# Multiplying feed-forward 0's first gate block for three token tiles before the fourth is turned

## The chip, the core and the metric

The kernel runs on one core of a Trainium2 chip. The metric is device time in microseconds (us), the median of the runs; smaller is better. The work is spread over TensorE (PE in the profile; PEld is its weight load), VectorE (DVE), ScalarE (ACT), GpSimd (POOL) and the DMA queues, which SyncE (SP) issues to here.

## What is computed

Two batches of 512 tokens, 512 channels wide, go through four layers, each in the form x = x + layernorm(layer(layernorm(x))). Only the first two matter here. Cut to them:

```python
# layer 0: a state space model, 1024 channels x 16 states, over 512 time steps
state = state * exp(dt_t * A) + (dt_t * u_t) * B_t      # for every t
y     = sum over the 16 states of state * C_t
y     = (y + x * D) * silu(gate);  out = y @ W_out.T
x     = x + layernorm(out)

# feed-forward 0: weights unpacked from 4-bit words, 512 -> 1376 -> 512
h     = layernorm(x)
inter = silu(h @ Wg) * (h @ Wu);   out = inter @ Wd
x     = x + layernorm(out)
```

Attention and a second feed-forward with latent experts follow. All matrix products are in f32.

## The kernel before

**The scan stage.** A batch is held as four token tiles of 128 tokens. The state space model is computed by blocks of 128 channels, eight for each batch, and for two of the 16 states at a time. That gives 16 blocks times 8 pairs of states, 128 steps, numbered s in the loop at L1152; gi is the pair within a block. A step has on DVE times_B (L1092, makes the input of step s+1), then scan (L1096, the recurrence); on ACT exps (L1076, the decay of step s+2, into one of two buffers `das`); on POOL times_C (L1102, and for some steps L1104, which adds the two states into one); and on PE sums (L1124), which adds up the states by products with the identity, two steps later. With gi of 2, fin (L1130) takes the sum of the block before, on DVE.

**Work beside the scan.** While batch 1 is scanned, PE also does batch 0's way out of the layer and its feed-forward 0 up to the product gate times up. This is a generator, `stream` (L1030). Out of it come, in this order: the output projection (`out_tiles`, L990), the turning of the normalised rows into channels by transposes (`turned`, L832), and `ffn0` (L1012). `ffn0` goes over 11 blocks of 128 columns. For each it multiplies gate (fg) and then up (fu), with four matmul calls each, since 512 channels are four chunks of 128. A call of f32 is two PE instructions.

**A plan written at trace time.** The order of instructions on PE, ACT, DVE and POOL is that in which the Python code issues them: `pin` (L407) ties every instruction to the one before it on its engine. The order comes from bookkeeping in the loop. Every step gives PE a credit of STEP = 3.5, of which at most MM = 0.86 is carried over from the step before (L1155). `sums` costs 0.86 for each product, a matmul call of the stream 0.86, a tile's transposes 0.43. While credit is above zero, the loop takes the next piece from the generator; a piece that has to wait yields `None`, and then nothing more is taken in that step.

**Jobs and ticks.** What follows a product on the other engines is a job, started with `spawn(job, lag)` and run when the count `now` has gone on by the lag. A step has two ticks: the first comes before times_B, the second between times_B and scan. So a job that runs in the second tick of step s puts its DVE instruction just ahead of scan(s), and its ACT instructions just ahead of exps(s+2). The jobs that matter:

- `turned`'s `out` (L843): the copy of one turned tile from the PSUM bank into hT, on ACT; lag 1 for the last two tiles.
- `ffn_gate_job` (L1000), after fg with lag 2: three ACT instructions by `silu_of` (L722 to L724), then a step later one POOL product (L727), which sets `st["it", i]`.
- `ffn_up_job` (L1006), after fu with lag 2, and not before `st["it", i]` + 2: one DVE product (L1009), called it(i) below.

**Banks.** PE's products of the stream share two PSUM banks in turn (`bank`, L738): one is given only when the last but one taken has been released. `dt_job` (pv, once for each block) takes a turn as well.

**Weights.** `gu_weights` (L366) loads 256 columns of gate and of up, 512 KB each, on SP's queue into a ring of three buffers. SP is not one of the pinned engines.

Of the kernel before, what the change touches and what calls it, by code (L numbers as in the profile page):

```python
# [18 lines left out]
P = 128  # L19
B = 2  # L20
S = 512
H = 512
NT = B * S // P
TB = S // P
KH = H // P
# [31 lines left out]
def tile_sandwich(  # L57
# [5 lines left out]
    nc = tc.nc  # L63
# [300 lines left out]
    hTs, o16 = {}, {}  # L364

    def gu_weights(b, j):  # L366
        cols = slice(j * PW, min((j + 1) * PW, INTER))
        n = cols.stop - cols.start
        return [w4(wgu_d[:, a, :, cols], f"w{nm}{b}_{j}", KH, n) for a, nm in enumerate("gu")]
# [29 lines left out]
    def xT_tile(name):  # L399
        return xTp.tile([P, KH, S], F32, tag="xT", name=name)  # L400
# [27 lines left out]
    with ExitStack() as mamba:  # L428
# [41 lines left out]
        def w_in(part, b, c):  # L470

            key = "w", part, b, c // 2
            if key not in st:
                st[key] = w4(W_in[part * NCH // 2 + c // 2], f"w_{'xg'[part]}{b}_{c // 2}")
            return st[key]
# [103 lines left out]
        with ExitStack() as p1:  # L579
# [5 lines left out]
            def bank1(i, name):  # L585
                return mbank(name) if i % 2 else ps_1.tile([P, S], F32, tag="mm", name=name)
# [3 lines left out]
            for i in range(TB + 2):  # L590
# [4 lines left out]
                if 0 <= i - 1 < TB:  # L595
                    j = i - 1
# [18 lines left out]
            for c in range(NCH):  # L615
                w = w_in(0, 0, c)
                ps = bank1(c, f"px0_{c}")
# [65 lines left out]
        with ExitStack() as p2:  # L683
# [13 lines left out]
            for n in range(NG):  # L697
                nc.tensor.matmul(
                    B0[:, n, :], pick[R_B : R_B + N_ST, n, :], st["bc"][R_B : R_B + N_ST],
                    start=True, stop=True,  # L700
# [7 lines left out]
            def spawn(gen, lag=0):  # L708
                jobs.append([now[0] + lag, gen])
# [25 lines left out]
            def release(name):  # L735
                next(t for t in turns if t[0] == name)[1] = now[0]

            def bank(name):  # L738
                while not bank_free():
                    yield None  # L740
                turns.append([name, None])
                return mbank(name)

            MM = 0.86
# [14 lines left out]
            def gate(b, c):  # L759
                w = w_in(1, b, c)  # L760
                if c + 2 - c % 2 < NCH:
                    w_in(1, b, c + 2 - c % 2)
                if (b, c) == (0, 1):
                    turns.append([f"pg{b}_{c}", None])
                    ps = first_gate
                    yield from in_proj(b, ps, w, c % 2, KH - 1)
                else:
                    ps = yield from bank(f"pg{b}_{c}")
                    yield from in_proj(b, ps, w, c % 2)
                spawn(gate_job(b, c, ps), 2)  # L770
# [16 lines left out]
            def proj_x(c):  # L787
                w = w_in(0, 1, c)
                if c + 2 - c % 2 < NCH:
                    w_in(0, 1, c + 2 - c % 2)  # L790
                while now[0] < 2 * (NGI * (c - 3) + 4):
                    yield None
                ps = yield from bank(f"px1_{c}")
                yield from in_proj(1, ps, w, c % 2)
                spawn(x_job(c, ps), 2)

            def until(key, lag):
                while st.get(key, 1 << 30) + lag > now[0]:
                    yield None
# [29 lines left out]
                    st[name, i] = now[0]  # L829
                    st[name, i, "xn"] = xn  # L830

            def turned(name, dst):  # L832

                for i in range(TB):
                    lag = 1 if name == "f0" and i >= TB - 2 else 2
                    yield from until((name, i), lag)
                    tp = yield from bank(f"tp_{name}_{i}")
                    tp = tp.rearrange("p (k t) -> p k t", k=KH)
                    for kc in range(KH):
                        nc.tensor.transpose(tp[:, kc, :], st[name, i, "xn"][:, ts(kc, P)], ident)  # L840

                    def out(i=i, tp=tp):
                        nc.scalar.copy(dst[:, :, ts(i, P)], tp)  # L843
                        release(f"tp_{name}_{i}")
                        st[name, i, "free"] = st[name, "out"] = now[0]
                        yield 1

                    spawn(out(), lag)
                    yield MM / 2
                for i in range(TB):  # L850
                    while (name, i, "free") not in st:
                        yield None

# [8 lines left out]
            def ranks1():  # L862
                yield from until(("u1", NCH - 1), 3)
                pm = yield from bank("psm1")
                pm = pm[:, : TB * N_ROW].rearrange("p (i r) -> p i r", i=TB)
                for i in range(TB):
                    for c in range(NCH):
                        ranks_of(1, c, i, pm)
                        if c % 4 == 3:
                            yield MM  # L870
                spawn(ranks1_job(pm), 2)

            def rows1():
                yield from until("nb1", 1)
                pt = yield from bank("pt1")
                ranks_rows(1, pt)

                def out():
                    ranks_out(1, pt)
                    release("pt1")  # L880
                    st["rows1"] = now[0]
                    yield 1

                spawn(out(), 2)
                yield MM / 2
# [66 lines left out]
            def fc1_expert():  # L952

                fT = w4(fc1_wT.rearrange("p k (a n) -> p (k a) n", n=PW), "wf1T")
                fT = fT.rearrange("p (k a) n -> p k (a n)", k=LAT // P)
                ex = w4(expert_w, "wex", LAT // P, LAT)
                for a in range(KH // 2):
                    ps = yield from bank(f"pfe{a}")
                    for e in range(2):
                        for k in range(LAT // P):  # L960
                            nc.tensor.matmul(
                                ps[:, ts(e, LAT)], fT[:, k, ts(2 * a + e, P)], ex[:, k, :],
                                start=(k == 0), stop=(k == LAT // P - 1),
                            )
                        yield MM

                    def out(a=a, ps=ps):
                        t_ = trow(f"fe{a}")
                        nc.scalar.copy(t_, ps)
                        release(f"pfe{a}")  # L970
                        nc.sync.dma_start(
                            out=wfe_d[:, 2 * a : 2 * a + 2, :].rearrange("p k n -> p (k n)"), in_=t_
                        )
                        yield 1

                    spawn(out(), 2)
# [35 lines left out]
            def ffn0():  # L1012

                hT = hTs["f", 0]
                wt = {0: gu_weights(0, 0)}
                for i, m in enumerate(IC):
                    j, e = divmod(i, 2)
                    for a, job in enumerate((ffn_gate_job, ffn_up_job)):
                        ps = yield from bank(f"f{'gu'[a]}0_{i}")
                        for kc in range(KH):  # L1020
                            nc.tensor.matmul(  # L1021
                                ps[:m], wt[j][a][:, kc, e * P : e * P + m], hT[:, kc, :],
                                start=(kc == 0), stop=(kc == KH - 1),
                            )
                            yield MM
                        spawn(job(i, ps), 2)
                    if not e and j + 1 < NP:
                        wt[j + 1] = gu_weights(0, j + 1)

            def stream():  # L1030
                for c in range(1, NCH):
                    yield from gate(0, c)
                xT.append(xT_tile("xT1"))
                w_in(0, 1, 0)
                yield from turned("n1", xT[1])
                for c in range(NCH):
                    yield from proj_x(c)
                yield from until("words", 2)
                yield from gate(1, 0)
                yield from gate(1, 1)  # L1040
                yield from ranks1()
                yield from gate(1, 2)
                yield from gate(1, 3)
                yield from rows1()
                for c in range(NCH - 4, NCH):
                    yield from gate(1, c)
                yield from fc1_expert()
                yield from out_tiles()
                hTs["f", 0] = xT_tile("hT_f0")
                yield from turned("f0", hTs["f", 0])  # L1050
                yield from ffn0()

            def words_job():
# [144 lines left out]
        with ExitStack() as p3:  # L1198
# [9 lines left out]
            for j in range(NCH // 2):  # L1208
                w = wo_pair(1, 0, j)
                for e in range(2):  # L1210
                    c = 2 * j + e
                    for i in range(TB):
                        nc.tensor.matmul(
                            po[i], g[1][c][:, ts(i, P)], w[:, e, :],
                            start=(c == 0), stop=(c == NCH - 1),
# [9 lines left out]
            for i, m in enumerate(IC):  # L1225
                j, e = divmod(i, 2)
# [7 lines left out]
                for t in range(TB):  # L1234
                    nc.tensor.matmul(  # L1235
                        fo[t], its[i][:m, ts(t, P)], w[:m, e],
                        start=(i == 0), stop=(i == len(IC) - 1),
# [279 lines left out]
```

## Time and profile before

| what | value |
|---|---|
| runs, us | 950.59, 951.03, 942.81; median 950.59 |
| the profiled execution, us | 950.37 |
| its span, first to last instruction, us | 948.4 |
| mean granted TensorE clock | 0.964 of full |
| busy share of the span: PE, DVE, ACT, POOL | 91%, 71%, 45%, 51% |
| scan stage, about 76 to 570 us: PE, DVE, POOL busy | 450.25, 472.83, 387.12 of 494 us |
| first products of feed-forward 0 (fg, fu at L1021) | 405.3 us to 559.7 us |

The profile is of one execution, 950.37 us by its own clock with a span of 948.4 us. A row of the timeline has start, length, engine, line, operation, output and inputs, shapes, count, and in brackets the idle time of the engine before it with what ended it. A row that merges pipelined matmuls is a little longer than the work in it, since the end of the last is modelled: eight instructions that start 0.43 us apart show as 3.60 us. Busy shares are averages over stages that have different limits, so a change in one stage has to be read in that stage.

### The profile page before, as it was taken

Reading aid. Unit: us, or ns where it says so; the run is one execution under the profiler, and the core shown is the slowest. Engines: PE = TensorE matmul, PEld = TensorE weight load, DVE = VectorE, ACT = ScalarE, POOL = GpSimd, SP = SyncE. Lnnn points to the kernel's source line nnn. Section 1 sums busy time; section 2 is a strip of 40 time slices with the busy share of each in tenths; the row PEclk is TensorE's granted clock in tenths of the full one; section 3 lists DMA queues with packets and bytes.
Section 4 is the critical chain, followed back from the end, with each engine's and each line's share of the span. In section 5 each row is a group of like instructions: output and inputs, shape, how many; then the busy total and the mean of one; then the engine's idle time right before and its main releaser. Section 6 shows DMA issues by size and latency. Waiting matters only on the chain.

```text
span 948.4 us, 7168 instructions
## 1 busy us (share of the span) xinstructions
PE 862.0 (91%) x2188; PEld 386.8 (41%) x2188; DVE 670.2 (71%) x770; ACT 428.9 (45%) x654; POOL 487.1 (51%) x356
## 2 busy tenths in 40 slices
PE   6988978879999898799999989899999998999994
PEld 3433433323534343244444434345344444545441
DVE  5878999999999999999999976425600034525235
ACT  4367875665667655655656520215220014322122
POOL 7747887776887788767878774510000000011012
PEclk9998999889999999799999999999999999999998
DMA  6549011110004944000111013346113221100101
GB/s 206 197 145 361 22 45 31 38 38 23 23 25 158 320 154 155 22 22 23 44 45 31 17 61 125 105 139 220 56 48 88 57 88 46 66 12 22 56 0 44
DMA packets 43816, 80.08 MB, mean 84 GB/s; under 512 B 7774, under 2 KB 20937, under 8 KB 43778
## 3 DMA queue, kind: packets, MB, share of 16 engines
q1 hardware_dynamic: 41506, 73.64, 23.6%
q0 software_dynamic: 1984, 5.47, 1.6%
q10 hardware_dynamic: 288, 0.52, 0.2%
q8 instruction: 17, 0.28, 0.1%
q14 instruction: 21, 0.17, 0.1%
HBM read 68.37 MB, written 11.24 MB: 84 GB/s over the span
## 4 chain that ended last, share of the span: by engine, by line
PE 35%; DVE 31%; issue 14%; POOL 6%; ACT 5%; DMA 2%; SPq 1%; DVEq 0%; POOLq 0%; ACTq 0%
DVE bx L1096 12%; DVE bx L1092 9%; PE pup L1382 5%; PE py L1124 4%; PE fu L373 4%; PE fg L373 4%; PE pd L1445 4%; PE fo L1298 3%; DVE u L485 2%; POOL bx L1102 2%; PE fo L1235 2%; PE po L990 2%; PE pg L749 1%; PE pr L1413 1%; POOL w_d L329 1%
## 5 line engine op out<-in xcount | busy, mean ns | idle before, releaser
L1102 POOL TENSOR_TENSOR bx<-bx,C 128x1024 f32<-128x1024 f32 x128 | 302.5, 2364 | 102.5 <-DVE bx L1096 81.4
L1096 DVE TENSOR_TENSOR_SCAN bx<-da,bx 128x1024 f32<-128x1024 f32 x128 | 291.7, 2279 | 2.8 <-ACT da L1076 2.8
L1124 PE MATMUL py<-bx,ident 128*128 128x512 f32 x480 | 233.5, 615 | 26.1 <-POOL bx L1102 23.6
L1076 ACT ACTIVATE da<-dt,A 128x511 f32<-128x511 f32 x256 | 176.6, 691 | 146.9 <-DVE bx L1096 142.4
L1092 DVE TENSOR_TENSOR bx<-du,B 128x1024 f32<-128x1024 f32 x127 | 152.9, 1204 | 2.1 <-DVE du L1090 0.4
L1124 PEld LDWEIGHTS py<-bx,ident 128*128 128x128 f32 x480 | 91.1, 195 | 150.8 <-issue 96.4
L1311 DVE TENSOR_TENSOR it<-it,fu 128x512 f32<-128x512 f32 (+1 forms) x11 | 7.6, 688 | 77.4 <-PE fu L373 76.3
L387 POOL TENSOR_TENSOR sd<-ve,half 128x4 f16<-128x4 f16 x2 | 2.1, 1044 | 115.0 <-DVE ve L385 115.0
L749 PE MATMUL pg<-xT,w_g 128*128 128x512 f32 x114 | 56.0, 621 | 3.3 <-ACT dt L573 3.3
L1382 PE MATMUL pup<-hT_l,wup 128*128 128x512 f32 x128 | 57.2, 602 | 0.0
L1445 PE MATMUL pd<-wdn,hid 128*128 128x512 f32 x128 | 56.3, 601 | 0.0
L129 POOL TENSOR_TENSOR rs_lo<-ve_lo,mhalf 128x1 f32<-128x1 f32 x8 | 5.9, 743 | 78.0 <-DVE ve_lo L127 75.2
L1235 PE MATMUL fo<-wd,it 128*128 128x512 f32 (+1 forms) x88 | 40.0, 616 | 3.8 <-DMA wd<-wd_d 3.8
L1021 PE MATMUL fg<-hT_f,wg 128*128 128x512 f32 (+1 forms) x88 | 42.5, 594 | 0.0
L373 PE MATMUL fg<-hT_f,wg 128*128 128x512 f32 (+1 forms) x88 | 41.9, 615 | 0.7 <-ACT hT_f L173 0.7
L373 PE MATMUL fu<-hT_f,wu 128*128 128x512 f32 (+1 forms) x88 | 42.4, 625 | 0.0
L1021 PE MATMUL fu<-hT_f,wu 128*128 128x512 f32 (+1 forms) x88 | 40.4, 594 | 1.4 <-ACT dt L573 1.4
L485 DVE SCALAR_TENSOR_TENSOR u<-px,ch,u 128x511 f32<-128x511 f32 (+2 forms) x48 | 35.8, 747 | 6.5 <-ACT u L478 5.4
L1298 PE MATMUL fo<-wd,it 128*128 128x512 f32 (+1 forms) x88 | 39.9, 595 | 0.0
L1445 PEld LDWEIGHTS pd<-wdn,hid 128*128 128x128 f32 x128 | 24.9, 194 | 31.8 <-issue 31.2
L1310 ACT ACTIVATE it<-fg 128x512 f32<-128x512 f32 (+1 forms) x11 | 6.6, 597 | 67.4 <-PE fg L373 67.4
L1382 PEld LDWEIGHTS pup<-hT_l,wup 128*128 128x128 f32 x128 | 24.5, 195 | 28.8 <-issue 28.8
(243 smaller groups left out, 1167.9 us busy)
## 6 DMA issues: line engine op xcount, KB each, us to landing
wo<-in_W_outT SPq DMA_DIRECT2D x20, 512.0 KB
B<-scr SPq DMA_DIRECT2D x16, 512.0 KB
C<-scr SPq DMA_DIRECT2D x16, 512.0 KB
wg<-wgu_d SPq DMA_DIRECT2D x10, 512.0 KB
wu<-wgu_d SPq DMA_DIRECT2D x10, 512.0 KB
w_x<-in_W_in SPq DMA_DIRECT2D x8, 512.0 KB
wgu_d<-w_gu POOLq DMA_DIRECT2D x16, 256.0 KB, 2.4
w_g<-in_W_in SPq DMA_DIRECT2D x8, 512.0 KB
```

Source lines behind the costliest of these rows:

```text
L373: nc.tensor.matmul(ps[:m], w[:, kc, e * P : e * P + m], hT[:, kc, :], start=(kc == 0), stop=(kc == KH - 1),)
L749: nc.tensor.matmul(ps, w[:, k, ts(e, P)], xT[b][:, k, :], start=(k == 0), stop=(k == KH - 1))
L1021: nc.tensor.matmul(ps[:m], wt[j][a][:, kc, e * P : e * P + m], hT[:, kc, :], start=(kc == 0), stop=(kc == KH - 1),)
L1076: nc.scalar.activation(das[s % 2][:, i, 1:], st["dt", b, c][:, 1:], AF.Exp, scale=A[:, c, n : n + 1])
L1092: nc.vector.tensor_mul(bx, st["du"].unsqueeze(1).to_broadcast([P, NG, S]), Bbs[b][gi])
L1096: nc.vector.tensor_tensor_scan(flat, das[s % 2].rearrange("p n t -> p (n t)"), flat, 0.0, ALU.mult, ALU.add)
L1102: nc.gpsimd.tensor_mul(bxs[s], bxs[s], Cbs[b][s % NGI])
L1124: nc.tensor.matmul(st["y"], ident, bx[:, i, :], start=False, stop=last)
L1235: nc.tensor.matmul(fo[t], its[i][:m, ts(t, P)], w[:m, e], start=(i == 0), stop=(i == len(IC) - 1),)
L1298: nc.tensor.matmul(fo[t], its[i][:m, ts(t, P)], w[:m], start=(i == 0), stop=(i == len(IC) - 1),)
L1382: nc.tensor.matmul(ps, w[:, kc, ts(e, P)], src[kc], start=(kc == 0), stop=(kc == KH - 1))
L1445: nc.tensor.matmul(pd, hid[kc][:, ts(i, P)], wdn[kc], start=(kc == 0), stop=(kc == INT // P - 1),)
```

## The change

`turned` takes a list of tiles, and `stream` calls it for the first three tiles only. In `ffn0`, gate's block 0 (i = a = 0) is cut in two: first the four matmul calls for tokens 0 to 383, then the fourth tile is turned, then the four calls for tokens 384 to 511, into the same bank. All other blocks stay as they were. The credit of a call goes by its width: 0.645 and 0.215 for these two kinds.

```diff
-            def turned(name, dst):
-
-                for i in range(TB):
+            def turned(name, dst, tiles=range(TB)):
+
+                for i in tiles:
                     lag = 1 if name == "f0" and i >= TB - 2 else 2
...
-                for i in range(TB):
+                for i in tiles:
                     while (name, i, "free") not in st:
                         yield None
...
                         ps = yield from bank(f"f{'gu'[a]}0_{i}")
-                        for kc in range(KH):
-                            nc.tensor.matmul(
-                                ps[:m], wt[j][a][:, kc, e * P : e * P + m], hT[:, kc, :],
-                                start=(kc == 0), stop=(kc == KH - 1),
-                            )
-                            yield MM
+
+                        t3 = (TB - 1) * P
+                        cuts = [(0, t3), (t3, S)] if i == a == 0 else [(0, S)]
+                        for t0, t1 in cuts:
+                            if t0:
+                                yield from turned("f0", hT, [TB - 1])
+                            for kc in range(KH):
+                                nc.tensor.matmul(
+                                    ps[:m, t0:t1], wt[j][a][:, kc, e * P : e * P + m], hT[:, kc, t0:t1],
+                                    start=(kc == 0), stop=(kc == KH - 1),
+                                )
+                                yield MM * (t1 - t0) / S
                         spawn(job(i, ps), 2)
...
-                yield from turned("f0", hTs["f", 0])
+                yield from turned("f0", hTs["f", 0], range(TB - 1))
                 yield from ffn0()
```

## The prediction

> **What bounds the kernel now.** First the page's groups by cost, for what the scan stage lives on.
>
> ```profile
> L1096 DVE TENSOR_TENSOR_SCAN bx<-da,bx 128x1024 f32<-128x1024 f32 x128 | 291.7, 2279 | 2.8 <-ACT da L1076 2.8
> L1092 DVE TENSOR_TENSOR bx<-du,B 128x1024 f32<-128x1024 f32 x127 | 152.9, 1204 | 2.1 <-DVE du L1090 0.4
> ```
>
> After the bar stand busy time, mean ns, and idle time before. The two DVE groups make 445 of the stage's 494 us, with next to no idle before them: DVE sets the pace. From 396 us to the last scan the trace has only two waits on DVE worth a line, and both stand before it(i), L1009. A later start of one scan is a later end, unless a wait behind it shrinks.
>
> Next TensorE around the edit, by the timeline, and its clock, by the busy table (stretch, its length, then PE's busy us; PEclk is the third number from the end).
>
> ```profile
> 396.19 2.07 PE L1119 MATMUL py<-u,dg 128*128 128x512 f32 x2 [1.65 <-DVE g L1130]
> 398.06 5.25 PE L1124 MATMUL py<-bx,ident 128*128 128x512 f32 x8
> 403.15 0.60 PE L840 MATMUL tp_f<-ident,xn_f 128*128 128x128 f32 x4
> 405.30 3.60 PE L1021 MATMUL fg<-hT_f,wg 128*128 128x512 f32 x8
> ...
> 413.89 1.88 PE L1021 MATMUL fu<-hT_f,wu 128*128 128x512 f32 x4
> ```
>
> ```profile
> 391.00:396.00 5.00, 2.29 (x6) 0.71 (x4) 4.90 (x7) 4.51 (x6) 3.38 (x4) 0.51 0.00 0
> 396.00:401.00 5.00, 4.81 (x6) 2.16 (x7) 5.00 (x5) 3.99 (x6) 3.46 (x2) 0.50 0.00 0
> ```
>
> The plan of before has an empty slot of PE ahead of the last tile's transposes: step 83 leaves 2.21 of credit, of which 0.86 is carried, so 1.35 is lost. The trace has no such hole. After the wait for fin (L1130) that ends at 396.19, PE runs without a pause past 424, and at half clock up to about 401. It is behind its plan, and DVE then waits 1.21 us for it, before it(0).
>
> Then ACT and DVE in the same place.
>
> ```profile
> 403.78 0.59 ACT L843 COPY hT_f<-tp_f 128x512 f32<-128x512 f32 x1 [2.87 <-PE tp_f L840]
> 404.27 1.42 ACT L1076 ACTIVATE da<-dt,A 128x511 f32<-128x511 f32 x2
> ```
>
> ```profile
> 407.12 2.28 DVE L1096 TENSOR_TENSOR_SCAN bx<-da,bx 128x1024 f32<-128x1024 f32 x1
> ...
> 410.43 2.28 DVE L1096 TENSOR_TENSOR_SCAN bx<-da,bx 128x1024 f32<-128x1024 f32 x1
> 412.63 0.67 DVE L1090 TENSOR_TENSOR du<-u,du 128x512 f32<-128x512 f32 x1
> 413.44 1.23 DVE L1092 TENSOR_TENSOR bx<-du,B 128x1024 f32<-128x1024 f32 x1
> 415.87 0.69 DVE L1009 TENSOR_TENSOR it<-it,fu 128x512 f32<-128x512 f32 x1 [1.21 <-PE fu L1021]
> 416.48 2.28 DVE L1096 TENSOR_TENSOR_SCAN bx<-da,bx 128x1024 f32<-128x1024 f32 x1
> ```
>
> Counted back from the last scan (562.64, s = 127), the three scans are s = 85, 86 and 87. it(0) stands ahead of scan(87).
>
> Last the end of the stage.
>
> ```profile
> 557.68 2.28 DVE L1096 TENSOR_TENSOR_SCAN bx<-da,bx 128x1024 f32<-128x1024 f32 x1
> 562.03 0.68 DVE L1009 TENSOR_TENSOR it<-it,fu 96x512 f32<-96x512 f32 x1 [2.07 <-POOL it L727]
> 562.64 2.28 DVE L1096 TENSOR_TENSOR_SCAN bx<-da,bx 128x1024 f32<-128x1024 f32 x1
> ```
>
> ```profile
> 559.52 1.26 POOL L1104 TENSOR_TENSOR bx<-bx 128x512 f32<-128x512 f32 x1
> 560.74 1.26 POOL L727 TENSOR_TENSOR it<-ti,it 96x512 f32<-96x512 f32 x1
> ...
> 565.06 2.34 POOL L1102 TENSOR_TENSOR bx<-bx,C 128x1024 f32<-128x1024 f32 x1 [0.76 <-DVE bx L1096]
> ```
>
> The last it, it(10), holds the last scan back by 2.07 us, because its POOL part comes late.
>
> **The change, part by part.** *The instructions.* Block 0 of gate costs PE the same columns. A pass over 512 takes 0.43 us from start to start, so one over 384 takes 0.32. For 128 columns the nearest row is the transposes, 128 columns with a weight load each: from 403.15 to 403.58, 0.108 us each, just a quarter of 0.43. So the eight more instructions cost nothing (8 x 0.108 = 0.86, as before). Were each at the 0.19 us of a weight load in the trace, they would cost 0.7 us more; I take 0. Loads move nowhere: SP sent the first two weight blocks at 371.1 and 372.8 us, long before.
>
> *The order in the plan*, worked out by hand from the credit. Step 83 has 2.64 left after its sums. Four calls at 0.645 leave 0.06, which is above zero, so the last tile is turned in the same step, behind them (left: -0.37). Step 84: 3.5 - 0.37 - 1.72 = 1.41, less four calls at 0.215 = 0.55. Then up's bank is asked for; the last but one taken is now fg's own, which is not released, so PE's stream stops and 0.55 is carried. Gate's job runs one step earlier. Step 85: 2.33 left after sums, three calls of up, -0.25. Step 86: 1.53, the fourth call of up, 0.67 left, and being above zero this lets the generator go on and spawn up's job in step 86. Before, up's fourth call was in step 86 too, but ended at -0.68, so its job was spawned in step 87. So **it(0) moves one step forward, ahead of scan(86), while the matmul that it waits for is in the same step as before.**
>
> *PE in time.* Nothing can start before 403.15, as everything up to there is the same and ahead in the queue. Then: gate's first part 8 x 0.32 = 2.57 to 405.72, transposes 0.43 to 406.15, then the sums, gate's second part and up. The work up to up's end is the same (12 us for 28 full passes), so up ends where it did, and it(0) starts at 415.87 as before.
>
> *ACT.* The copy of the last tile keeps its place in ACT's queue, but its transposes come 2.57 us later: it starts at 406.35. Behind it waits exps(85), which then runs 406.84 to 408.26, so scan(85) starts at 408.3 and not at 407.12: 1.2 us on DVE. Behind exps(85) are gate's three ACT instructions and exps(86), which nobody needs before it(0) anyway.
>
> *DVE.* scan(85) at 408.3, times_B at 410.5, and at 411.6 DVE stands before it(0), which it can start at 415.87: a wait of 4.2 us, in which the 1.2 us disappear. Queued behind it are scan(86) (2.20 us to the next start), L1090 (0.81) and times_B (1.13), which ran ahead of it before. scan(87) starts at 416.48 + 2.20 + 0.81 + 1.13 = 420.6 and not at 416.48: **4.1 us later**. times_C and sums of step 86 wait with it; PE idles some 2 us at 420 to 425, which takes nothing from the end as long as DVE sets the pace.
>
> *Given back at the end.* Carried on to the last block, the same bookkeeping spawns gate's last job at the beginning of step 123; its POOL part falls in step 124, ahead of times_C(124), where POOL has 0.95 us idle on either side, and it(10) before scan(126). The 2.07 us on DVE go, and of POOL's end 1.26 us of L727 leave the row from 559.52: add to 560.78, times_C(126) to 563.13, times_C(127) to 565.5, instead of starting at 565.06 and ending at 567.4. **1.9 us earlier** relative to the rest. What follows 570 us is the same chain moved.
>
> *Between* (425 to 560 us), it(1), it(4), it(5) and it(7) come in the step of their own up product. I find it(1)'s fu done 0.7 us ahead of DVE. Together they may cost 0 to 1 us; I take 0.
>
> **Sum**: 4.1 - 1.9 = +2.2 us on the profiled 950.37 (span 948.4 to 950.6). The profiled execution is 0.2 us under the median of the runs, so 950.59 + 2.2 = 952.8.
>
> *A rule against the trace.* The Trainium skill, "TensorE: Matmul & The Clock Gate", section "The HAM clock gate (the 'warmup' mystery)", has the clock halved after an idle window of about 3.4 us. No gap of PE here is over 1.7 us from 386 to 396, yet the table shows 0.51 and 0.50, with PE busy under half of 391 to 396. By the rule alone PE would have run at full clock, 2.6 us earlier at 403.15; then before would not have waited for up (415.87 - 2.6 is ahead of DVE's 414.66), after would wait from 410.4 to 413.3, and the loss would be 2.9 - 1.9 = +1.0. I take the trace's half clock; the rule's value is the low end of this case. The high end is +5: half clock again after PE's new idle time, and the 1 us of the later it.
>
> **The rivals.** *A, the slot was real*: PE fills idle time, up ends earlier and the 1.21 us go, with the end's 1.9: -3.1, 947.5. For it speaks the plan's 1.35 of lost credit; against it that PE has no gap from 396.19 on.
>
> *B, it(0) stays ahead of scan(87)* because I have misjudged a spawn by one step: then the 1.2 us at scan(85) vanish in the old wait of 1.21, and only the end remains: -1.9, 948.7. Speaks for it that the deciding credits, 0.06 and 0.67, are small.
>
> *C, slower by over 1%: PE becomes the bound.* From 425 to 560 it is busy 132.5 of 135 us. Spare are 2.5 us and the 4.1 by which DVE is late. Half clock for 10 us, as at 391 to 401, costs 5 and stays hidden; it decides from 13 us on, and 30 us cost 15 - 6.6 = 8.4, in all +10.6, 961.2. Against it: the clock fell where PE was busy half of the time, while after the edit it is busy over three quarters.
>
> **How the numbers follow.** The forecast 0.62, A 0.15, B 0.15, C 0.08 (of it 0.03 over 1%). The likeliest's own range is +1 to +5: 951.6 to 955.6. The three runs shown differ by 0.9%, with one at 942.81; a median there would give 945. The range of 945 to 957 takes in A, B and that, and leaves out most of C. About 1% is what a measurement tells from no change: faster 0.02, same 0.95, slower 0.03.
>
> **What would show it.** In the changed kernel's timeline: fg in forms 128x384 and 128x128; the tile's copy on ACT waiting some 5.4 us for PE; DVE's it(0) with a wait near 4 us for fu and scan(86) behind it; no wait before the last it; the last scan near 564.6 instead of 562.64. A wait before it(0) under 2 us would refute the main step; PE idle between 396 and 403 would speak for A; a last it still waiting for POOL takes back the 1.9; PEclk at 0.5 past 405 speaks for C.

## The result, and the profile after

| | us |
|---|---|
| changed, median of 20 runs | 950.15 (946.01 to 952.79) |
| before, median of 20 runs, on the same chip | 945.18 (941.12 to 951.03) |
| ratio, with its 95% interval | 1.0049 (1.0033 to 1.0065) |
| profiled execution of the changed kernel, its span | 952.62, 950.5 |

The change makes the kernel 0.5% slower, some 4.6 us on 945 (3.1 to 6.1). That is under the 1% taken as clear, but the interval excludes no change. The three runs of before that stood ahead of the prediction, median 950.59, lay high; the difference has to be read from the ratio.

In the changed kernel's file the lines behind `ffn0` stand six lower: scan is L1102, times_B L1098, sums L1130, fin L1136, the stream's products L1027. In the profiled execution, step 84's scan starts at 401.74, 2.07 us earlier than before. That comes from the start of the stage: from the first scan to that of step 8 the traces of this document took 31.5 to 34.3 us, though the kernels are the same up to there. So times are compared from scan(84).

DVE in the place of the edit, by the timeline of the changed kernel:

```profile
406.70 2.29 DVE L1102 TENSOR_TENSOR_SCAN bx<-da,bx 128x1024 f32<-128x1024 f32 x1 [1.57 <-ACT da L1082]
...
414.31 0.69 DVE L1009 TENSOR_TENSOR it<-it,fu 128x512 f32<-128x512 f32 x1 [4.21 <-PE fu L1027]
414.92 2.28 DVE L1102 TENSOR_TENSOR_SCAN bx<-da,bx 128x1024 f32<-128x1024 f32 x1
...
418.97 2.28 DVE L1102 TENSOR_TENSOR_SCAN bx<-da,bx 128x1024 f32<-128x1024 f32 x1
```

The three scans are 85, 86 and 87. it(0) now stands ahead of scan(86) and waits 4.21 us there, for the same product of PE for which it waited 1.21 us ahead of scan(87). PE and ACT in the same place:

```profile
401.55 2.74 PE L1027 MATMUL fg<-hT_f,wg 128*128 128x384 f32 x8
404.13 0.60 PE L840 MATMUL tp_f<-ident,xn_f 128*128 128x128 f32 x4
404.56 1.88 PE L1130 MATMUL py<-bx,ident 128*128 128x512 f32 x4
406.28 1.05 PE L1027 MATMUL fg<-hT_f,wg 128*128 128x128 f32 x8
...
413.19 1.02 PE L1027 MATMUL fu<-hT_f,wu 128*128 128x512 f32 x2
```

```profile
404.76 0.59 ACT L843 COPY hT_f<-tp_f 128x512 f32<-128x512 f32 x1 [5.92 <-PE tp_f L840]
405.25 1.42 ACT L1082 ACTIVATE da<-dt,A 128x511 f32<-128x511 f32 x2
```

From start to start the eight passes over 384 columns take 2.58 us, and the eight over 128 take 0.90. On ACT the copy of the last tile waits 5.92 us for its transposes, and exps(85) stands behind it; that is the 1.57 us ahead of scan(85).

The end of the stage: DVE, then PE, then the busy table for 571 to 574 us. In the table the stretch, its length and PE's busy us come first; the third number from the end is PEclk, the granted clock.

```profile
563.04 0.67 DVE L1009 TENSOR_TENSOR it<-it,fu 96x512 f32<-96x512 f32 x1
563.63 4.46 DVE L1102 TENSOR_TENSOR_SCAN bx<-da,bx 128x1024 f32<-128x1024 f32 x2
575.10 0.69 DVE L1136 TENSOR_TENSOR g<-g,py 128x512 f32<-128x512 f32 x1 [7.01 <-PE py L1130]
```

```profile
565.89 1.12 PE L1130 MATMUL py<-bx,ident 128*128 128x512 f32 x2 [2.44 <-POOL bx L1110]
568.45 6.61 PE L1130 MATMUL py<-bx,ident 128*128 128x512 f32 x8 [1.44 <-POOL bx L1108]
```

```profile
571.00:574.00 3.00, 3.00 (x5) 1.28 (x4) 0.00 (x0) 0.00 (x0) 0.00 (x0) 0.50 0.15 26
```

it(10) has no wait any more, and the last two scans follow each other. But PE does the last sums, eight passes, in 6.6 us, nearly all of it at half clock, and the last fin waits for them.

### The profile page after: what moved, and what is told of

Its sections match the earlier page's. It is cut to its first block, busy times and chain, and to the rows that moved or that the text cites. A ratio compares the mean times of both kernels' runs of the same rounds, so it can differ in the third digit from the quotient of the medians.

```text
span 950.5 us, 7184 instructions
## 1 busy us (share of the span) xinstructions
PE 864.7 (91%) x2196; PEld 387.8 (41%) x2196; DVE 669.9 (70%) x770; ACT 429.0 (45%) x654; POOL 485.9 (51%) x356
## 4 chain that ended last, share of the span: by engine, by line
PE 44%; DVE 28%; issue 12%; POOL 4%; ACT 4%; DMA 2%; SPq 1%; DVEq 0%; POOLq 0%; ACTq 0%
DVE bx L1102 10%; PE py L1130 8%; DVE bx L1098 8%; PE pd L1451 6%; PE pup L1388 5%; PE fu L373 3%; PE fo L1304 3%; PE fg L373 3%; PE fu L1027 2%; DVE u L485 2%; PE po L990 2%; PE pg L749 2%; PE fo L1241 2%; PE pr L1419 1%; PE fg L1027 1%
## 5 line engine op out<-in xcount | busy, mean ns | idle before, releaser
L1102 DVE TENSOR_TENSOR_SCAN bx<-da,bx 128x1024 f32<-128x1024 f32 x128 | 291.6, 2278 | 1.9 <-ACT da L1082 1.8
L1130 PE MATMUL py<-bx,ident 128*128 128x512 f32 x480 | 237.5, 625 | 29.0 <-POOL bx L1108 23.6
L1130 PEld LDWEIGHTS py<-bx,ident 128*128 128x128 f32 x480 | 92.1, 199 | 157.1 <-issue 92.9
L1098 DVE TENSOR_TENSOR bx<-du,B 128x1024 f32<-128x1024 f32 x127 | 152.9, 1204 | 2.6 <-DMA B<-scr 0.6
L1027 PE MATMUL fu<-hT_f,wu 128*128 128x512 f32 (+1 forms) x88 | 43.5, 618 | 1.1 <-ACT dt L573 1.1
L1027 PE MATMUL fg<-hT_f,wg 128*128 128x512 f32 (+3 forms) x96 | 41.4, 557 | 0.0
L373 PE MATMUL fg<-hT_f,wg 128*128 128x512 f32 (+1 forms) x88 | 40.2, 593 | 0.7 <-ACT hT_f L173 0.7
```

Of the source, the lines that this page charges most:

```text
L373: nc.tensor.matmul(ps[:m], w[:, kc, e * P : e * P + m], hT[:, kc, :], start=(kc == 0), stop=(kc == KH - 1),)
L1027: nc.tensor.matmul(ps[:m, t0:t1], wt[j][a][:, kc, e * P : e * P + m], hT[:, kc, t0:t1], start=(kc == 0), stop=(kc == KH - 1),)
L1098: nc.vector.tensor_mul(bx, st["du"].unsqueeze(1).to_broadcast([P, NG, S]), Bbs[b][gi])
L1102: nc.vector.tensor_tensor_scan(flat, das[s % 2].rearrange("p n t -> p (n t)"), flat, 0.0, ALU.mult, ALU.add)
L1130: nc.tensor.matmul(st["y"], ident, bx[:, i, :], start=False, stop=last)
```

## The experiments

Three theories were held against each other. *Theory 1*: what costs the time is the place of it(i) in DVE's order, a step ahead of PE. *Theory 2*: it is the late turning of the fourth tile and the cut products. *Theory 3*: it is PE falling to half clock in new places.

Single executions scatter by some us outside the scan stage. So beside the ratio each trace is read from the start of scan(84) to the start of the last fin, in four stretches. All in us; "half" counts PE's 512-wide passes at half clock between scan(125) and the last fin.

| kernel | scan 84 to 87 | 87 to 125 | 125 to 127 | to last fin | sum | half | ratio (95%) |
|---|---|---|---|---|---|---|---|
| before | 12.67 | 137.89 | 8.27 | 7.40 | 166.2 | 3 | |
| changed | 17.23 | 140.76 | 6.11 | 9.27 | 173.4 | 7 | 1.0049 (1.0033 to 1.0065) |
| changed, again | 15.65 | 139.05 | 6.11 | 9.32 | 170.1 | 7 | 1.0045 (1.0028 to 1.0062) |
| it(0) forward only | 16.97 | 137.92 | 8.26 | 7.21 | 170.4 | 4 | 1.0043 (1.0023 to 1.0062) |
| cut only | 13.31 | 137.88 | 8.26 | 7.52 | 167.0 | 3 | 1.0004 (0.9983 to 1.0024) |
| it(0) back | 11.99 | 140.82 | 6.11 | 8.81 | 167.7 | 7 | 1.0005 (0.9988 to 1.0022) |
| changed, kept busy | 16.99 | 140.76 | 6.11 | 6.95 | 170.8 | 0 | 1.0016 (0.9998 to 1.0034) |
| it(0) back, kept busy | 13.21 | 140.82 | 6.11 | 6.94 | 167.1 | 0 | 0.9996 (0.9974 to 1.0019) |
| before, two waits | 10.77 | 139.89 | 8.32 | 6.84 | 165.8 | 0 | 0.9979 (0.9961 to 0.9997) |
| before, last product early | 12.01 | 137.87 | 6.09 | 7.51 | 163.5 | 0 | 0.9969 (0.9953 to 0.9984) |
| the same, kept busy | 11.88 | 137.91 | 6.09 | 7.52 | 163.4 | 0 | 0.9964 (0.9948 to 0.9979) |

### One instruction forward, in the kernel before

```diff
-                while ("it", i) not in st or now[0] < st["it", i] + 2:
+                while ("it", i) not in st or now[0] < st["it", i] + (2 if i else 0):
...
+                            if a and not i and kc == KH - 1:
+                                spawn(job(i, ps), 2)
                             yield MM
-                        spawn(job(i, ps), 2)
+                        if i or not a:
+                            spawn(job(i, ps), 2)
```

> The kernel before, with one instruction moved: it(0) on DVE stands ahead of scan(86), as in the changed kernel, instead of ahead of scan(87). PE, ACT and POOL keep their order; nothing is cut or turned later. Theory 1 (the order on DVE costs the time): it(0) still waits for up's block 0, which ends at about the same place, and scan(86), L1090 and a times_B come after the wait: +4.1 us over before, ratio about 1.0043, with a wait of some 5.4 us ahead of it(0) in the profile. Theory 2 (the late turning and the cut products cost it): nothing of that is here, so no difference from before. Theory 3 (PE falls to half clock in new places): no difference that can be named in advance, within 1 us of before.

Measured: ratio 1.0043 (1.0023 to 1.0062). DVE's timeline of this run:

```profile
409.29 1.19 DVE L1095 TENSOR_TENSOR bx<-du,B 128x1024 f32<-128x1024 f32 x1
416.09 0.69 DVE L1009 TENSOR_TENSOR it<-it,fu 128x512 f32<-128x512 f32 x1 [5.61 <-PE fu L1021]
416.70 2.28 DVE L1099 TENSOR_TENSOR_SCAN bx<-da,bx 128x1024 f32<-128x1024 f32 x1
```

it(0) starts at 416.09, about where it did before (415.87), with a wait of 5.61 us (5.4 expected). The stretch from scan 84 to 87 is 4.3 us longer, and the others are as before. So this one move is enough for a loss of the change's size, with no tile turned later. Theory 2 isn't needed for it.

### The same instruction back, in the changed kernel

```diff
-                        spawn(job(i, ps), 2)
+                        spawn(job(i, ps), 4 if i == 0 and a else 2)
```

> The changed kernel, with one instruction moved: up's job of block 0 has lag 4 instead of 2, so it(0) stands ahead of scan(87), as before the change. All else is the changed order. Theory 1: the 4.1 us come back at it(0), but DVE then reaches it(1) and the later products some 4 us earlier while PE has no more time than it had, so part is lost again ahead of it(1), it(3) or it(5); with the 2 us won at the last block, +0 to +2.5 us over before, that is 2.5 to 5 us under the changed kernel. Theory 2: scan(85) still waits 1.5 us for exps(85) and the cut is still there, so it stays at the changed kernel's +5 us. Theory 3: stays within 1 us of the changed kernel.

Measured: 1.0005 (0.9988 to 1.0022), so most of the loss is gone, while the late turning and the cut are still in place. The first stretch comes back. The second stays 2.9 us longer than before, since DVE reaches it(1) earlier while PE does not. The waits ahead of it(1), here, and of it(5), 0.71, make up 2.6 of it:

```profile
424.71 0.69 DVE L1009 TENSOR_TENSOR it<-it,fu 128x512 f32<-128x512 f32 x1 [1.90 <-PE fu L1027]
```

### The cut alone

```diff
+                        t3 = (TB - 1) * P
+                        cuts = [(0, t3), (t3, S)] if i == a == 0 else [(0, S)]
+                        for t0, t1 in cuts:
...
                             yield MM * (t1 - t0) / S
```

> The kernel before, with gate's block 0 cut into four products of 384 and four of 128 tokens, but after the fourth tile is turned, as before. Prices the eight more PE instructions alone. Theory 1: each pass of 128 columns costs 0.11 us, a quarter of a full one, so no difference from before (0 to 0.7 us at most, ratio 1.000 to 1.0007). Theory 2, as far as it means the small products: up to the whole of the changed kernel's +5 us. Theory 3: no difference.

Measured: 1.0004 (0.9983 to 1.0024). The small products cost nothing that can be measured here, though the interval leaves room for some 2 us either way. The changed kernel's own rows price them more closely: 2.58 + 0.90 us for the sixteen passes, against 3.44 for eight whole ones at 0.43. (The bookkeeping put three of the four small calls behind the sums of step 83, so gate's ACT work came later; in the trace the wait of 1.21 us ahead of it(0) is replaced by one of 1.85 us ahead of the du of step 86, L1090 in the kernel before.)

### The changed kernel again

> The changed kernel itself, for a second trace and a time on the same chip as the other three. All theories: about +5 us over before (ratio 1.003 to 1.0065). Theory 1: a wait of 4 to 4.5 us ahead of it(0), about 3 us more ahead of it(3), it(5) and a du, and none ahead of the last it. Theory 3: the half clock stretches of PE near 568 to 574 us in the first trace are there again; theory 1 takes them for chance and expects the tail from the last scan to the last fin to differ from trace to trace by 1 to 2 us.

Measured: 1.0045 (1.0028 to 1.0062). Its trace has the 4.21 us ahead of it(0), but no wait of scan(85), and 1.7 us less in the second stretch. Both come from PE's clock. For scan(85) it is the passes at half clock behind the fin of step 82, seven in the first trace and three in this one. For the second stretch, here is the same place of PE's timeline, first in the changed kernel's first trace, then in this one:

```profile
457.34 5.40 PE L1027 MATMUL fu<-hT_f,wu 128*128 128x512 f32 x8 [1.10 <-ACT dt L573]
```

```profile
454.41 3.70 PE L1027 MATMUL fu<-hT_f,wu 128*128 128x512 f32 x8 [1.11 <-ACT dt L573]
```

After the same pause of 1.1 us the eight passes took 5.40 us in one execution and 3.70 in the other; why is taken up further down. In the first, DVE then waited 0.58 us ahead of it(3), 0.91 ahead of a du (L1096) and 0.94 ahead of it(5); in the second, 0.72 in all. As theory 3 had it, the half clock at the end of the stage is in both traces; I had taken it for chance.

### Keeping PE busy at the end

```diff
+                if s == NS - 1:
+                    spare = mbank("spare")
+                for _ in range({NS - 1: 2, NS: 1}.get(s, 0)):
+                    nc.tensor.matmul(spare, ident, u[1][NCH - 1], start=True, stop=True)
```

> The changed kernel, with three more products that nobody reads (identity by a finished block, into a spare bank) in PE's idle time at the end of the scan stage: two ahead of the sums of step 125, one ahead of those of step 126. They add no dependency to the chain. Theory 1, with the clock for the end: in the changed order PE has run out of stream work a step earlier, waits 2.4 and 1.4 us, and runs the last sums at half clock, which is why the 2.2 us won before the last scan are gone at the last fin. Kept busy it stays at full clock: from the last scan to the last fin 6.7 to 7.4 us instead of 9.3, and about +3 us over before instead of +5. Rival (POOL or the wait for it sets the tail, the clock is beside the point): 9.3 us stay and the time stays at +4 to +5.

Measured: 1.0016 (0.9998 to 1.0034). PE's last sums in this run:

```profile
567.42 1.13 PE L1130 MATMUL py<-bx,ident 128*128 128x512 f32 x2 [0.74 <-POOL bx L1110]
568.38 1.02 PE L1168 MATMUL spare<-u,ident 128*128 128x512 f32 x2
569.96 1.98 PE L1130 MATMUL py<-bx,ident 128*128 128x512 f32 x4 [0.56 <-POOL bx L1108]
572.27 1.98 PE L1130 MATMUL py<-bx,ident 128*128 128x512 f32 x4 [0.32 <-POOL bx L1108]
```

Four passes take 1.98 us again, no pass is at half clock, and the way from the last scan to the last fin is 6.95 us in place of 9.3. More work on PE made the chain shorter: the clock was what had eaten the gain at the end. The second stretch stays at 140.76, as in the first trace, because here too the eight passes behind the pause of 1.1 us took 5.40 us. (The ratio's interval still meets that of the changed kernel again, from 1.0028; it is the stretch that shows it.) With it(0) back as well:

> The changed kernel with it(0) back ahead of scan(87) and with the three products of the run before in PE's idle time. Theory 1 with the clock: both losses are undone, what stays is a wait of some 2 us ahead of it(1) against 2.2 us won before the last scan: tail 6.7 to 7.4 us, and -1 to -2.5 us against before (ratio 0.9975 to 0.999). Rival (the clock is beside the point): the same as it(0) back alone, tail 8.8, ratio about 1.0005.

Measured: 0.9996 (0.9974 to 1.0019). The tail is 6.94 us as expected, and the sum 167.1, but this is no measurable gain over before; the wait ahead of it(1) and two small ones (it(5) 0.70, scans 85 and 86 1.66 together) hold what was won. The interval, some -2.5 to +1.8 us, takes in the expected -1 to -2.5 as well as nothing, so the gain is not shown.

### The waits of before, taken away directly

```diff
-                        spawn(job(i, ps), 2)
+                        spawn(job(i, ps), 4 if i == 0 and a else 2)
...
+                if rows < P:
+                    nc.vector.tensor_mul(dst[:rows], th[:rows], dst[:rows])
+                    return
                 yield from pool_turn()
```

With it goes one spare product in each of the two places, by the same lines as in the kept busy run.

> The kernel before, its stream order untouched, with the two waits of DVE ahead of it(i) taken away directly: up's job of block 0 gets lag 4, so it(0) stands ahead of scan(88), and the last block's product of sigmoid and value is made by DVE instead of POOL, so that it(10) does not wait for POOL; one more product in PE's idle time ahead of each of the last but one and the last but two sums. Theory 1: what counts is where it(i) stands on DVE and whether PE and POOL are done by then: no wait ahead of it(0) (-1.2 us where there was one) and of it(10) (-2.07, less 0.6 for the product), tail 0 to 1 us shorter: -2 to -3.5 us against before, ratio 0.9963 to 0.998. Rival (DVE's waits are covered by other work): no difference.

Measured: 0.9979 (0.9961 to 0.9997), inside the expected range, but in the trace only a part of it comes out as expected. The first wait went, but 2.0 us came back behind it (it(0) itself now lies there, 0.6; fin waits 0.40, it(1) 0.81). The second went as well, but the product on DVE took its place. Here is POOL, then DVE:

```profile
553.78 2.36 POOL L1105 TENSOR_TENSOR bx<-bx,C 128x1024 f32<-128x1024 f32 x1 [1.24 <-DVE bx L1099]
554.38 2.30 DVE L727 TENSOR_TENSOR it<-ti,it 96x512 f32<-96x512 f32 x1
```

It took 2.30 us, where the product of the same size with one operand in PSUM (L1009) takes 0.68. The stage is 0.4 us shorter in this trace, and the tail alone, with its clock kept up, is 0.56 shorter.

So a last pair leaves DVE and PE as they are and moves one POOL instruction, the last block's product, ahead of times_C(125):

```diff
-                yield 2
+                if rows == P:
+                    yield 2
                 yield from pool_turn()
...
-                        spawn(job(i, ps), 2)
+                        spawn(job(i, ps), 4 if a and m < P else 2)
```

> The kernel before, with one POOL instruction moved: the last block's product of sigmoid and value stands ahead of times_C(125) instead of behind it and its addition, so that it(10) on DVE need not wait for POOL. DVE's order and PE's stay. Theory 1: the 2.07 us ahead of it(10) go and the last scan starts 2.1 us earlier relative to scan(84), but POOL has the same work to do up to the end, so the last fin comes only 1 to 1.5 us earlier; if PE falls to half clock earlier for it, less. From scan(84) to the last fin 165 us, ratio 0.998 to 1.000. Rival (POOL alone sets the end of the stage, and the order within it is all the same): nothing, 166.2 us or more.

Measured: 0.9969 (0.9953 to 0.9984). Of this kernel POOL, then DVE, then PE at the end:

```profile
554.00 1.27 POOL L728 TENSOR_TENSOR it<-ti,it 96x512 f32<-96x512 f32 x1 [0.54 <-ACT ti L724]
```

```profile
557.50 0.66 DVE L1010 TENSOR_TENSOR it<-it,fu 96x512 f32<-96x512 f32 x1
```

```profile
558.97 1.12 PE L1125 MATMUL py<-bx,ident 128*128 128x512 f32 x2 [1.64 <-POOL bx L1105]
561.27 1.98 PE L1125 MATMUL py<-bx,ident 128*128 128x512 f32 x4 [1.18 <-POOL bx L1103]
```

it(10) no longer waits, the stretch from scan(125) to scan(127) is 2.2 us shorter, and PE, whose stream ends where it did before, pauses 1.64 and 1.18 us and stays at full clock. This is the change's gain at the end without its loss, some 2.9 us under before (1.5 to 4.4), and more than the 1 to 1.5 that were expected, since the tail did not grow as feared. The same with PE kept busy (one spare product in each of the two places):

> The run before, with one more product that nobody reads in PE's idle time ahead of the sums of step 125, and one ahead of those of step 126, to keep its clock up. Theory 1 with the clock: no pass at half clock between scan(125) and the last fin, 0.5 to 1 us less than the run before: from scan(84) to the last fin some 164 us, -2 us against before, ratio 0.9965 to 0.9995. Rival (the clock at the end is worth nothing in this order): the same as the run before.

Measured: 0.9964 (0.9948 to 0.9979), the stage 163.4: the same as without. Another 0.5 to 1 us had been expected of the spare products, and that did not come: where PE did not fall to half clock there was nothing to win, as the rival had said for this order. These two runs are faster than the kernel before, and so than the changed one.

## Why the prediction came out as it did

The direction and the main step were right. The size, +2.2 us, was about half of the +4.6 measured and lies outside its interval of 3.1 to 6.1. The predicted time, 952.8, lies nearer, 2.7 us above the measured 950.15, but that is luck: it started from a median of before that was 5.4 us too high, and the two errors partly cancel.

- *The order in the plan*: right. it(0) stands ahead of scan(86), and up's last call is in the same step as before. One move of that instruction makes a loss of the same size (1.0043), and moving it back takes most of it away (1.0005).
- *DVE, 4.1 us later*: right in kind and size. The wait was 4.21 us, predicted 4.2; from scan 84 to 87 the two traces of the changed kernel took 4.56 and 2.98 us more than before. The two differ by PE's clock up to scan(84), with seven passes at half clock after fin in one and three in the other, as the two values 4.1 and 2.9 of the prediction had it.
- *ACT*: right. The copy waited 5.92 us (5.4 predicted) and scan(85) 1.57 us (1.2), all inside the wait of it(0).
- *The instructions cost nothing*: right as far as it can be measured: 1.0004 for the cut alone, and 3.48 us for the sixteen passes.
- **"Given back at the end ... 1.9 us earlier relative to the rest"**: the step that failed. On DVE it came, 2.16 us between scan(125) and scan(127), and on POOL too: its last times_C ends 2.06 us earlier after scan(125) than before. In the second trace the last scan starts just the 2.0 us later after scan(84) that were forecast. But at the last fin nearly all that was given back was gone, since the stretch from the last scan was 1.87 and 1.92 us longer. Because the stream ended earlier, PE stood 2.44 and 1.44 us with 1 us of work between, and did seven of the last eight passes at half clock (first trace). All three traces with this stream order and no spare products have seven such passes; before, it(0) forward and the cut alone have three or four; three spare products removed them. I had moved POOL's end forward and taken PE's speed as given.
- **"Together they may cost 0 to 1 us; I take 0"**: too small. The later stretch cost 1.2 us in one trace and 2.9 in the other. The waits are ahead of it(1), it(3), it(5) and a du; the 1.7 us between the two traces are the half clock after a pause of 1.1 us.

Put together for the first trace: 4.56 + 2.87 - 2.16 + 1.87 = 7.1; for the second 2.98 + 1.16 - 2.16 + 1.92 = 3.9. The ratio's 4.6 lies between.

Of the rivals, A fell: PE has no pause between fin's end and the fourth tile's transposes in either trace. B fell with the order. C in its form (PE the bound for tens of us) did not come, but its mechanism was at work in small.

*When the clock falls.* The prediction weighed a rule of the Trainium skill, "TensorE: Matmul & The Clock Gate", section "The HAM clock gate (the 'warmup' mystery)", and read its idle window of about 3.4 us as the length of a pause. So read it would have let PE run on, since no pause at the end is over 2.45 us, yet the clock was 0.50. The same section has the window free-running, and with that the traces agree. In the first trace of the changed kernel the clock is at half from 393.43 to 400.26 us, from 458.29 to 461.70 and from 567.51 to 574.34. The distances between these six times are 2, 17, 1, 31 and 2 steps of 3.41 us, and between 300 and 600 us every change of the clock in the eleven traces fits such a grid of its own. Here are two steps at the end of the changed kernel, then two of the kernel with the last product early, in the busy table:

```profile
564.10:567.51 3.41, 1.12 (x2) 0.30 (x2) 3.41 (x2) 0.00 (x0) 3.11 (x3) 1.00 0.10 38
567.51:570.92 3.41, 2.47 (x3) 1.18 (x4) 0.58 (x1) 0.00 (x0) 3.19 (x2) 0.50 0.00 0
```

```profile
555.37:558.79 3.42, 1.97 (x5) 0.49 (x3) 3.42 (x4) 0.35 (x1) 3.34 (x2) 1.00 0.14 15
558.79:562.20 3.41, 2.05 (x4) 0.78 (x5) 1.57 (x1) 0.00 (x0) 3.41 (x3) 1.00 0.38 144
```

From scan(125) to the last fin six traces fell to half clock, each behind a step with PE busy for 1.13 us or less; in the five that did not fall, no whole step has less than 1.84. So what counted there was PE's work within a step, not the longest pause. The grid also goes with the pause of 1.1 us. It is in all five traces with the changed stream order. In two of them (the first, and the changed kernel kept busy) the pause and the small products pv ahead of it lie in one step, and the clock fell. In the other three a border between steps cuts the pause or pv, and it did not fall. PE was busy for 2.31 us in that step of the first trace, more than in steps at the end that passed, so its busy time alone is not the whole rule. No run moved a pause against the grid, so this is read from the traces and not tested. Another section of that page, "A second HAM failure mode: psum-queue depth-cycling", tells of short idle times between groups of bf16 products that let the clock swing; no run here tells that case from this one.

## What to carry to other kernels

In an order fixed by hand, work moved ahead is no gain if the engine that feeds it has no free time in the execution: an empty slot in the plan is not an idle engine in the trace. Look at where the consumer lands in the busiest engine's queue; if it moves ahead and its producer does not, the whole distance becomes a wait. And when a producer runs dry early, count its clock: here the pieces that were left ran at half speed, on the chain.

## What the runs showed of the hardware that was not expected

- Spare products on PE made the stage shorter: 6.95 us from the last scan to the last fin against 9.3, with no other change, and 6.94 against 8.81 with it(0) back.
- Between 300 and 600 us the granted clock changed only on a grid of 3.41 us, and at the stage's end it fell behind each step in which PE was busy for 1.13 us or less, although no pause was over 2.45 us.
- A DVE product of two SBUF operands, 96x512 f32, took 2.30 us when it started 0.6 us into a POOL product of 2.36 us, and ended 0.5 us after it. The like with one operand in PSUM takes 0.68. Two SBUF operands alone are not the reason: L1429 of the kernel before, 128x512, takes 0.69 with POOL idle. This is what the Trainium skill, "SBUF — State Buffer", section "SBUF: two separate sides", says of the port pair that the two engines share: an exclusive lock, where the loser waits for the whole instruction. One instance agrees with it here; the wait itself is not a row of the trace, but lies inside the 2.30 us.
